# Scheduling ranks in a four-layer macaron network: routings and layer 0's attention 150 places ahead

## The chip, the cores and the metric
The kernel runs on one core of a Trainium2 chip. A core has five engines with a queue of instructions each: PE (TensorE, matmuls, with its weight loads shown as PEld), DVE (VectorE), ACT (ScalarE), POOL (GpSimd, which here issues the indirect gathers and scatters) and SP (SyncE, which issues the plain DMAs). The metric is the device time of one execution in microseconds (us), as the median over runs.

## The reference
Four sequences (batches 0 to 3) of 1024 tokens with 128 channels go through four layers, all in fp32. Each layer adds half a feed-forward block, an attention, and the same feed-forward block again. What matters here is layer 0 and layer 2, whose feed-forward blocks are mixtures of eight experts with two taken per token:

```python
x = x + 0.5 * _L0_ffn_ref(_layernorm(x), router_w, w1, b1, w2, b2)     # routed, GELU
x = x + _L0_attn_ref(_layernorm(x), Wq, Wk, Wv, Wfc)
x = x + 0.5 * _L0_ffn_ref(_layernorm(x), router_w, w1, b1, w2, b2)
x = x + 0.5 * _L1_ffn_ref(...)                                         # dense, SiLU
x = x + _L1_attn_ref(...)
x = x + 0.5 * _L1_ffn_ref(...)
x = x + 0.5 * _L2_ffn_ref(...)                                         # routed, ReLU
x = x + _L2_attn_ref(...)
x = x + 0.5 * _L2_ffn_ref(...)
...
# the routed block
logits = xf @ router_w.T
top_vals, top_idx = top_k(logits, 2); probs = softmax(top_vals)
for e in range(8):
    w = sum(where(top_idx == e, probs, 0))
    out += w * (act(xf @ w1[e].T + b1[e]) @ w2[e].T + b2[e])
# layer 0's attention: 16 heads of 8 channels, softmax over the heads of one token, not over tokens
scores = einsum('bshd,bstd->bsht', Q, K) / sqrt(8)
out = einsum('bsht,bstd->bshd', softmax(scores), V) @ Wfc.T
```

Layer 2's attention is a linear recurrence with a decay, layer 1's a softmax over 1024 tokens, layer 3 a recurrent mixer.

## The kernel before
The residual of each batch stays on the chip with channels on partitions (`X[b]`, 128x1024). A routed block is done in three kinds of tasks for a group of one or two batches.

- *Routing* (`route`, lines 276 to 421): normalizes the group's tokens, writes them as rows to DRAM (line 307), finds the two experts of each token, counts, and works out for every slot of every block which row it takes (`g_source`) and where its result goes (`g_target`, line 412, the last instruction). It is a chain of some 55 small DVE instructions, with matmuls and ACT work between. The eight `g_lanes` steps (line 399), with four matmuls each, are near its end.
- *Experts* (`experts`, lines 424 to 474): 23 blocks of 128 slots for one batch, 39 for two. For each block SP loads the expert's weights (`e_w`, four buffers), POOL gathers 128 rows (`e_xg`, line 457), PE transposes them (line 461), DVE copies them (`e_x`, line 463), PE multiplies up, ACT applies the activation (`e_h`, line 468), PE multiplies down, DVE adds the bias (`e_y`, line 441) and POOL scatters the result to DRAM (line 442).
- *Combine* (`combine`, lines 476 to 498), per batch: loads the two results of each token back (`c_y`, line 487), weighs and adds them (lines 492 and 493), transposes them (line 496) and adds half of them to the residual.

Layer 0's attention of a batch (`l0_attn`, lines 501 to 572) works on eight tiles of 128 tokens; each tile has four large DVE operations of 128x2048 elements (lines 528, 530, 545, 547) and some small ones, between a projection and a transposition on PE. Tasks are named after the round (0 before, 1 after the attention) and their first batch: route00, experts02, combine03. `middle0` to `middle3` are the attentions, `first` and `last` the dense feed-forward of layer 1 that is done inside the layers 0 and 2. In layer 0 the groups are (0), (1), (2, 3) in the first round and (0, 1), (2), (3) in the second; in layer 2 they are (0, 1) and (2, 3) both times.

The order of the work arises in two steps. `lanes` (line 1188) lays the tasks of several lanes out in turns: it always continues the lane whose clock of estimated costs is lowest, and begins a task when the tasks that it names are done. In layer 0 the lanes are: all experts; all combines; first routings, attentions and last feed-forwards; second routings. Then a list scheduler sets the order in each engine's queue at build time: among the instructions that it sees as ready it takes the one that was laid out first. The order in a queue is fixed from then on; semaphores do the waiting. Work of the routings, combines and attentions writes to the four PSUM banks of the pool `side`, the experts to the four of `main` (the first routing of each layer excepted).

Layer 1's attention has an order of PE written out by hand. The change does not touch it, nor layer 3.

Of the kernel before, what the change touches and what calls it, by code (L numbers as in the profile page):

```python
# [205 lines left out]
class Macaron:  # L206
# [981 lines left out]
    def lanes(self, *lanes):  # L1188
        lanes = [list(lane) for lane in lanes]
        clock, active, done = [0.0] * len(lanes), [None] * len(lanes), set()  # L1190
        while any(lanes) or any(active):
# [13 lines left out]
            else:  # L1205
                clock[n] += cost

    def macaron(self, name, moe, func, groups, marks, more):


        weights, (side, main), wp = self.packs[name + "m"], (self.side, self.main), self.fp
        plans = {}

        def plan(n, group):
            return plans.setdefault((n, group), {"mark": marks[n, group]})

        def route(n, group, *after, ps=side):
            return f"route{n}{group[0]}", after, lambda: self.route(ps, wp, moe, group, plan(n, group))

        def experts(n, group):  # L1220
            names = (f"route{n}{group[0]}",)
            return f"experts{n}{group[0]}", names, lambda: self.experts(main, wp, weights, func, group, plan(n, group))

        def combine(n, group):
            for b in group:
                yield f"combine{n}{b}", (f"experts{n}{group[0]}",), lambda b=b: self.combine(side, wp, group, b, plan(n, group))

        every = [(n, group) for n in range(2) for group in groups[n]]
        blocks = [experts(*g) for g in every]
        back = [task for g in every for task in combine(*g)]  # L1230
        self.lanes(blocks, back, *more(route))

    def layer0(self, moe, m, right, enter, ffn):
        m["wqkvc"] = self.centered(m["wqkv"], 3 * D)
        pa, pf = enter(right, "l0a"), enter(right, "l1f0")
        side, main = self.side, self.main

        def more(route):
            attn = lambda b, *after: (f"middle{b}", after, lambda: self.l0_attn(side, pa, m, b))
            last = lambda b, ps: (f"last{b}", (f"combine1{b}",), ffn(pf, ps, b))  # L1240
            return (
                [
                    route(0, (0,), ps=main), route(0, (1,)), route(0, (2, 3)),
                    *[attn(b, f"combine0{b}") for b in range(B)],
                    last(0, side), last(1, side), last(2, side), last(3, main),
                ],
                [route(1, (0, 1), "middle0", "middle1", "combine03"), route(1, (2,), "middle2"), route(1, (3,), "middle3")],
            )


        groups = [(0,), (1,), (2, 3)], [(0, 1), (2,), (3,)]
        marks = {(0, (0,)): "_1", (0, (1,)): "_2", (0, (2, 3)): "_0", (1, (0, 1)): "_0", (1, (2,)): "_1", (1, (3,)): "_2"}
        self.macaron("l0", moe, AF.Gelu, groups, marks, more)
# [118 lines left out]
```

## Time and profile before

| what | us |
|---|---|
| median of 3 runs | 3209.11 (3207.99 to 3214.21) |
| the profiled execution | 3296.3, its span 3294.4, mean granted PE clock 0.905 |
| layer 0 | from 0 to 945 |
| layer 1's attention | from 945 to 2038 |
| layer 2 | from 2038 to 2806 |
| layer 3 | from 2806 to the end |

The tasks of layers 0 and 2 in this execution, by the first and last DVE instruction of each:

| layer 0 | us | layer 2 | us |
|---|---|---|---|
| experts00 | 50 to 145 | route00 | 2098 to 2154 |
| experts01 | 143 to 235 | experts00 | 2159 to 2291 |
| middle0 | 177 to 300 | route02 | 2150 to 2215 |
| experts02 | 233 to 387 | experts02 | 2290 to 2451 |
| middle1 | 313 to 427 | route10 | 2431 to 2476 |
| combine03 | 407 to 413 | combine03 | 2480 to 2489 |
| route10 | 442 to 515 | experts10 | 2480 to 2647 |
| middle2 | 434 to 567 | route12 | 2602 to 2650 |
| experts10 | 517 to 670 | experts12 | 2654 to 2781 |
| middle3 | 582 to 729 | combine13 | 2798 to 2802 |
| route12 | 595 to 644 | | |
| experts12 | 667 to 783 | | |
| route13 | 756 to 791 | | |
| experts13 | 797 to 898 | | |

Whole-span busy shares are averages over stretches with different limits, and the kernel does little that the whole span could explain. The stretch is the unit to read: which engine is busy in it, and for what the engine that should be busy waits. The page's 40 slices show where such stretches begin:

```profile
PE   6888637878879999999999999988988977899997
DVE  3376877774226676676776772431555521355664
PEclk7989858889977999999999999979989988788997
```

Each digit is the busy share of 82 us in tenths, in the last row the PE clock that was granted.

### The profile page before, as it was taken

The page shows a single profiled execution, that of the slowest core. Times are in us where ns is not written, and L with a number is a line of the kernel's source. Part 1 is how long each engine was busy: PE and PEld are TensorE (multiplying, and loading weights), DVE is VectorE, ACT ScalarE, POOL GpSimd, SP SyncE. Part 2 cuts the span into 40 slices and gives each one's busy share as a digit, 9 for nine tenths or more (in the row PEclk, how much of TensorE's full clock was granted, in tenths as well). Part 3 has the DMA queues.
Part 4 walks back from the last instruction along what each step waited for, and adds up shares of the span by engine and source line. Part 5 has one row for each costly group of instructions (what it writes and reads, how often), then busy time and mean ns, then how long its engine had stood idle before and what let it go on. Part 6 is the DMA issues. An engine that isn't in the chain of part 4 may idle for free.

```text
span 3294.4 us, 48535 instructions
## 1 busy us (share of the span) xinstructions
PE 2875.3 (87%) x18206; PEld 1685.8 (51%) x18206; DVE 1826.5 (55%) x3160; ACT 1649.2 (50%) x3640; POOL 807.0 (24%) x748
## 2 busy tenths in 40 slices
PE   6888637878879999999999999988988977899997
PEld 6766426766643333333333333586777865344333
DVE  3376877774226676676776772431555521355664
ACT  3565524658613565566566565444444534444442
POOL 2565405552340000000000000046434454011110
PEclk7989858889977999999999999979989988788997
DMA  4766414663500000000000000157565666000000
GB/s 151 227 186 188 140 42 130 185 188 115 168 9 7 4 6 4 6 6 4 21 5 6 1 1 9 42 152 245 171 185 147 199 197 194 0 0 0 7 7 13
DMA packets 122890, 277.64 MB, mean 84 GB/s; under 512 B 18016, under 2 KB 67296, under 8 KB 122528
## 3 DMA queue, kind: packets, MB, share of 16 engines
q1 hardware_dynamic: 101792, 231.77, 23.8%
q0 software_dynamic: 20864, 42.77, 4.3%
q8 instruction: 144, 2.36, 0.3%
q14 instruction: 90, 0.74, 0.1%
HBM read 238.43 MB, written 31.85 MB: 82 GB/s over the span
## 4 chain that ended last, share of the span: by engine, by line
PE 74%; DVE 12%; ACT 5%; issue 4%; DMA 3%; POOL 1%; another core or an unknown queue 0%; SPq 0%; ACTq 0%; DVEq 0%; POOLq 0%
PE bank L227 40%; PE two L227 17%; PE o L227 8%; PE s L227 4%; DVE nm L720 2%; ACT e_h L468 2%; PE wave L1010 1%; DVE prod L545 1%; PE bank L461 1%; DMA c_y<-res 1%; DVE sc L530 1%; ACT L468 1%; DMA e_w<-in_l0m_dram 1%; DVE prod L528 1%; DVE e_x L463 1%
## 5 line engine op out<-in xcount | busy, mean ns | idle before, releaser
L720 DVE TENSOR_REDUCE nm<-two 128x2 f32<-128x1024 f32 x512 | 626.9, 1225 | 288.3 <-PE s L227 268.9
L743 ACT ACTIVATE e<-s 128x512 f32<-128x512 f32 x1024 | 556.4, 595 | 405.6 <-PE s L227 402.6
L468 ACT ACTIVATE e_h<-bank,e_w 128x128 f32<-128x128 f32 x1304 | 454.8, 368 | 511.6 <-PE bank L227 388.4
L227 PE MATMUL bank<-e_x,e_w 128*128 128x128 f32 x2608 | 569.3, 318 | 154.5 <-ACT e_h L468 79.9
L227 PE MATMUL s<-qm,kz 32*128 32x512 f32 x2048 | 634.1, 643 | 0.8 <-ACT e L743 0.8
L227 PE MATMUL two<-kz,qz 32*128 32x512 f32 x2048 | 593.2, 664 | 21.3 <-DVE nm L720 2.5
L227 PEld LDWEIGHTS bank<-e_x,e_w 128*128 128x128 f32 x2608 | 413.9, 204 | 291.3 <-ACT e_h L468 144.4
L457 POOL DMA_INDIRECT e_xg<-rows,g_source x326 | 334.4, 1026 | 835.1 <-DVE g_target L412 354.2
L227 PE MATMUL bank<-e_w,e_h 128*128 128x128 f32 x2608 | 445.7, 291 | 12.3 <-ACT e_h L468 6.9
L442 POOL DMA_INDIRECT res<-e_y,g_target x326 | 373.5, 1146 | 337.0 <-DVE e_y L441 152.7
L227 PEld LDWEIGHTS bank<-e_w,e_h 128*128 128x128 f32 x2608 | 378.8, 205 | 23.0 <-ACT e_h L468 13.3
L227 PE MATMUL o<-e,va 128*32 128x256 f32 x4096 | 328.8, 392 | 0.1
L441 DVE TENSOR_TENSOR e_y<-bank,e_w 128x128 f32<-128x128 f32 x326 | 94.3, 290 | 403.7 <-PE bank L227 317.0
L227 PEld LDWEIGHTS two<-kz,qz 32*128 32x128 f32 x2048 | 159.7, 189 | 239.9 <-issue 164.0
L227 PEld LDWEIGHTS o<-e,va 128*32 128x32 f32 x4096 | 81.0, 108 | 390.3 <-issue 370.3
L227 PEld LDWEIGHTS s<-qm,kz 32*128 32x128 f32 x2048 | 206.9, 183 | 10.9 <-issue 7.7
L708 POOL COPY va<-vd 128x256 f32<-128x256 f32 x16 | 6.7, 433 | 626.3 <-PE o L227 538.0
L1115 POOL TENSOR_TENSOR z<-st,r 128x512 f32<-128x512 f32 x32 | 46.2, 1445 | 417.1 <-DVE st L1108 333.7
L463 DVE COPY e_x<-bank 128x128 f32<-128x128 f32 x326 | 93.0, 285 | 92.2 <-PE bank L461 67.6
L227 PE MATMUL bank<-g_cols,g_lanes 128*128 128x39 f32 (+1 forms) x512 | 90.5, 341 | 28.9 <-DVE g_cols L392 28.8
L461 PE MATMUL bank<-c,e_xg 128*128 128x128 f32 x326 | 95.0, 291 | 21.7 <-DMA e_xg<-rows,g_source 21.6
L227 PEld LDWEIGHTS bank<-g_cols,g_lanes 128*128 128x128 f32 x512 | 91.2, 270 | 32.5 <-issue 31.4
(300 smaller groups left out, 3694.0 us busy)
## 6 DMA issues: line engine op xcount, KB each, us to landing
e_w<-in_l0m_dram SPq DMA_DIRECT2D x170, 578.0 KB
e_w<-in_l2m_dram SPq DMA_DIRECT2D x156, 578.0 KB
c_y<-res SPq DMA_DIRECT2D x32, 512.0 KB
rows<-g_xt SPq DMA_DIRECT2D x16, 512.0 KB
e_xg<-rows,g_source POOLq DMA_INDIRECT x326
res<-e_y,g_target POOLq DMA_INDIRECT x326
x<-in_x_dram SPq DMA_DIRECT2D x4, 512.0 KB
qz<-qd SPq DMA_DIRECT2D x64, 32.0 KB
```

The lines of the kernel that those rows point to most:

```text
L227: self.nc.tensor.matmul(out, lhsT, rhs, start=start, stop=stop)
L441: nc.vector.tensor_tensor(y, o, w[:, MOE_W - D :], ALU.add)
L442: ins = nc.gpsimd.indirect_dma_start(out=res[:, :], out_offset=at(target[:, k : k + 1]), in_=y, in_offset=None)
L457: nc.gpsimd.indirect_dma_start(out=xg, out_offset=None, in_=rows[:, :], in_offset=at(source[:, k : k + 1]))
L461: nc.tensor.transpose(tp, xg, self.c0["ident"])
L463: nc.vector.tensor_copy(x, tp)
L468: nc.scalar.activation(h[:, fc, :], up[:, fc, :], func, bias=w[:, 2 * FC * P + fc : 2 * FC * P + fc + 1])
L528: v.tensor_tensor(pr, q.unsqueeze(2).to_broadcast(sh), k.unsqueeze(1).to_broadcast(sh), ALU.mult)
L530: v.tensor_reduce(sc, pr, AX.X, ALU.add)
L720: v.tensor_reduce(nm[:, it, h, 2 * pair : 2 * pair + 2], s, AX.X, ALU.max, negate=True)
L743: nc.scalar.activation(es[g], s, AF.Exp, scale=scale)
L1115: (pool if i else v).tensor_tensor(z, st[:, 0:HALF], r, ALU.mult)
```

## The change
A helper wraps a task so that every step of it is laid out under a rank 150 places ahead of where it stands: the scheduler treats its instructions as though they had been laid out 150 instructions earlier. Two kinds of tasks are wrapped: all routings (layers 0 and 2), and layer 0's attentions. Experts, combines, layer 2's attentions and the dense feed-forwards keep their places. A block of the experts is some 19 instructions, so 150 places are nearly eight blocks. `lanes` itself lays out the same sequence as before, since the wrapper hands the costs through.

```diff
+    def ahead(self, task, offset):
+
+        while True:
+            with self.tc.high_priority(offset=offset):
+                cost = next(task, None)
+            if cost is None:
+                return
+            yield cost
+
     def macaron(self, name, moe, func, groups, marks, more):
...
         def route(n, group, *after, ps=side):
-            return f"route{n}{group[0]}", after, lambda: self.route(ps, wp, moe, group, plan(n, group))
+            return f"route{n}{group[0]}", after, lambda: self.ahead(self.route(ps, wp, moe, group, plan(n, group)), 150)
...
         def more(route):
-            attn = lambda b, *after: (f"middle{b}", after, lambda: self.l0_attn(side, pa, m, b))
+            attn = lambda b, *after: (f"middle{b}", after, lambda: self.ahead(self.l0_attn(side, pa, m, b), 150))
```

## The prediction

> **What bounds the kernel now.** The page comes first, and its 40 slices show two stretches that can move at all: layer 0 (0 to 945 us) and layer 2 (2038 to 2806 us). Layer 1's attention between them is ordered by hand, and layer 3 keeps its order: of its DVE instructions one moves, by two places.
>
> Second view, the busy time of each engine by stretch. Columns: stretch, length, busy us (instructions) of PE, PEld, DVE, ACT and POOL, granted PE clock, DMA share, GB/s.
> ```profile
> 177.00:427.00 250.00, 175.62 (x1040) 140.70 (x1040) 200.29 (x294) 140.28 (x325) 135.81 (x104) 0.86 0.54 164
> 427.00:515.00 88.00, 42.42 (x167) 34.01 (x165) 62.90 (x97) 23.06 (x72) 1.96 (x2) 0.54 0.12 40
> 515.00:797.00 282.00, 228.74 (x1369) 186.57 (x1370) 187.55 (x381) 182.52 (x421) 152.70 (x127) 0.90 0.59 175
> 2080.00:2159.00 79.00, 77.58 (x340) 55.63 (x338) 35.65 (x88) 38.97 (x113) 3.87 (x4) 0.85 0.16 53
> 2159.00:2291.00 132.00, 109.88 (x740) 95.62 (x738) 37.48 (x132) 59.89 (x175) 79.67 (x80) 0.94 0.70 211
> 2450.00:2480.00 30.00, 17.10 (x77) 15.68 (x76) 16.59 (x45) 4.91 (x16) 4.97 (x5) 0.54 0.51 158
> 2645.00:2660.00 15.00, 7.55 (x46) 6.54 (x46) 3.16 (x12) 1.72 (x6) 8.80 (x9) 0.68 0.67 185
> ```
> From 177 to 427 us (attention of batches 0 and 1 beside the experts) DVE is the limit, 200 of 250 us. From 427 to 515 us no experts run: their next group waits for its routing, as POOL's gather queue says:
> ```profile
> POOL e_xg L457 <- DVE g_far L410: 124.7, 1, 124.7
> ```
> In layer 2 PE is the limit, with holes where a group of experts has ended and the next routing has not: 2450 to 2480 and 2645 to 2660 us, both at a low granted clock.
>
> Third view, groups of DVE rows from 177 to 427 us (busy, mean ns, idle before and its ender). A large attention operation is 2.2 to 2.3 us, an expert's copy or add under 0.3 us, and the add is what DVE waits at:
> ```profile
> L545 DVE TENSOR_TENSOR prod<-ex,qkv 128x2048 f32<-128x2048 f32 x16 | 35.8, 2240 | 0.0
> L441 DVE TENSOR_TENSOR e_y<-bank,e_w 128x128 f32<-128x128 f32 x56 | 15.9, 287 | 29.7 <-PE bank L227 29.5
> L463 DVE COPY e_x<-bank 128x128 f32<-128x128 f32 x54 | 15.4, 285 | 5.6 <-PE bank L461 5.3
> ```
> Fourth, DVE in order of time. The last add of an expert group, then the first multiply of the combine that reads that group: 11.8 us apart (batch 1), and 9.3 us (batch 2).
> ```profile
> 235.10 0.29 DVE L441 TENSOR_TENSOR e_y<-bank,e_w 128x128 f32<-128x128 f32 x1 [1.26 <-PE bank L227]
> 246.91 1.93 DVE L493 SCALAR_TENSOR_TENSOR c_y<-c_y,g_p,c_y 128x128 f32<-128x128 f32 x7 [1.32 <-DMA c_y<-res]
> ...
> 386.42 0.28 DVE L441 TENSOR_TENSOR e_y<-bank,e_w 128x128 f32<-128x128 f32 x1
> 395.68 1.66 DVE L493 SCALAR_TENSOR_TENSOR c_y<-c_y,g_p,c_y 128x128 f32<-128x128 f32 x6 [1.55 <-DMA c_y<-res]
> ```
>
> **What the Trainium skill says.** "Perfetto Trace Analysis", Sequencer Loop: an engine reads its next instruction, and that one waits for its semaphores. So the order built into a queue holds even where a later instruction is ready; the 29.5 us at L441 agree. The same page, Optimization Strategy: stretches with different most-contended engines gain by being interleaved; 427 to 515 us (DVE alone) is such a stretch. "TensorE: Matmul & The Clock Gate", What's actually happening: PE's clock falls to half after an idle window of about 3.4 us; the 0.54 at 2450 us agrees.
>
> **The change part by part.** Nothing is computed differently. DVE has 3160 instructions in both builds, PE 9490 matmuls, POOL 748; ACT table loads go from 203 to 198. What changes is the order in each queue, so I compared the built orders and summed, from the trace of before, the durations of what stands ahead of each milestone.
>
> *B, 177 to 427 us: +20 us.* On DVE, attention overtakes experts: ahead of experts01's last add stand 60.5 us of batch 0's attention (before: 43.9), ahead of experts02's last add 72.0 us of batch 1's (58.0). Work up to batch 1's last DVE instruction stays 290.3 us, counted from the start, of which 69.5 lie ahead of batch 0's first (now 68.2). So attention itself comes no earlier; experts come later. And combines are not ranked: in the new PE order the next attention matmuls stand directly behind combine01's transposes, since they share the four side banks. On DVE the order now reads: attention, then 14 expert instructions with no attention among them, then combine01, then attention. Price of this pause: about three blocks to experts01's last add at the pace of the 300 to 316 us stretch (5 copies in 16 us, 3.2 us each), 9.6 us, plus 11.8 us to the combine, minus 14 x 0.286 = 4.0 us of work: 17 us idle. Behind the waiting transposes PE's queue also holds experts02's next matmuls, so that group stands still for the end of the pause. The second pause, 10 expert instructions before combine02: 3.5 x 3.2 + 9.3 - 2.9 = 17 us. Against it: before, DVE idled 250 - 220.8 = 29 us (sum of durations); a third of the 29.7 us at L441 should go, as adds now stand further behind their matmuls (-10), and batch 0's first large operations follow at once on its reciprocal (-5). Idle 29 + 34 - 15 = 48, work 222, together 270 against 250. Bounds: +5 if blocks stand ready and each pause is half as long, +35 if nothing of the 15 comes back.
>
> *C, 427 to 515 us: -6 us.* Route10 ends behind the same 68 to 70 us of DVE work. Its third instruction started at 458, behind 14.8 us of work in 31 us: it waited. Now 29.1 us of attention stand ahead of it, which use that time; I put it at 39 us. The 40.6 us left, at the old pace (54.2 us took 57), take 43: 82 against 88. Bounds -10 and +4.
>
> *D, 515 to 797 us: -6 us.* Before, experts12's last add is at 782.9, route13's last instruction at 791.2 and experts13's first copy at 797.3. In the new order route13 ends ahead of experts12's last add, so 14 us become one block's pitch: -11. A third pause of 14 expert instructions (before combine10) and 18.7 us more DVE work ahead of experts10's last add cost, but that stretch has DVE busy 188 of 282 us, and experts run on in the pause: +5. The five table loads saved (1283 ns each by the trace, on an engine with slack) are counted at nothing. Bounds -14 and +8.
>
> *E, 2080 to 2291 us: -11 us.* Route00 took from 2084 (its first ACT instruction) to 2154; routings with PE nearly free took 56 (2420 to 2476) and 58 us (2592 to 2650). In the new order it stands ahead of the ffn, with 27 us less PE and 10.5 us less DVE work before its end: experts00 starts 12 us earlier. (PE work: each matmul at its mean busy time in layer 2's full-clock stretches, 0.34 us for an up-projection of an expert, 0.23 us for a down-projection.) About 26 us of PE work move into its 132 us, where PE was busy 110; it just fits, so +1. Bounds -20 and -4. SP's rows transfer of route02 drops behind ten weight loads; experts02 need it 100 us later.
>
> *F, 2291 to 2806 us: -11 us.* Route10's last 21 us (2454 to 2475) ran at the low clock between two combines. Now the last blocks of experts02 stand between its instructions and combine02 and combine03 behind it: PE keeps its clock, about -8. What was late becomes the combines, 13 us of PE work later, and with them batches 2 and 3; that nearly uses up the 7 us hole between experts10's last add (2646.5) and experts12's first copy (2653.9), which closes: -3. Bounds -20 and -2.
>
> Sum: 20 - 6 - 6 - 11 - 11 = -14 us on the profiled execution's 3296.3 us. That one is 87 us (2.7%) over the median of 3209.11; I take the difference over unchanged: 3195.
>
> **Rivals.** *Combines hold up attention for longer (slower).* One mechanism: attention ranked ahead delays the expert group whose combine it must then wait for in PE's order. For it: DVE is the limit in B, and no rank helps the combines. Against it: DVE has 29 us idle there now. With B at +35, D at +5 (third pause), C 0, E -8, F -7: +25, 3234. It decides once the two pauses leave DVE idle over 48 us together; up to there the gains of C to F cover it.
> *The pauses are covered (faster).* Blocks stand ready behind attention and run through fast: B 0, C -8, D -12, E -13, F -13: -46, 3163. For it: POOL and DMA are half idle in B. Against it: 9 to 12 us from last add to combine are waits for transfers, which no order shortens.
> *The order moves and the end does not.* Routings are chains of small steps with their own length (56 to 58 us), so E and F give 5 each and B takes 10: 3209. Against it: C, D and F have visible holes.
>
> **How the numbers follow.** Chances: forecast 0.49, own range 3180 to 3213; slower rival 0.31; covered pauses 0.14; no effect 0.06. A measurement tells 0.2% (6.4 us) from no change. Faster by more: 0.33 + 0.14 + 0.01 = 0.48; within: 0.12 + 0.01 + 0.04 = 0.17; slower: 0.04 + 0.30 + 0.01 = 0.35. The range 3163 to 3236 leaves out the outer half of each outer rival, about 0.2.
>
> **What would show it.** B: experts02's last add near 405 to 420 us (before 386), and two stretches without attention on DVE, ended by L493. C: route10 from barrier to end in 82 us. D: experts13's first copy within 4 us of experts12's last add. E: experts00's first copy near 2147 less the shift of layer 0. F: no slice with half clock between experts02 and experts10. It is wrong if B costs more than all the others give, or if experts00 of layer 2 does not start earlier.

## The result, and the profile after

| kernel | median us | runs | span of the profiled execution |
|---|---|---|---|
| before | 3210.51 (3207.99 to 3214.21) | 4 | 3294.4 |
| after | 3290.28 (3280.79 to 3291.35) | 4 | 3287.5 |

The ratio is 1.0241 [1.0219, 1.0263]: the change makes the kernel about 80 us slower. The two spans say the opposite, minus 7 us. The profiled execution of before took about 80 us more than its timed ones, as every execution of this kernel did on the chip of experiments e1 to e4, nearly all of it where experts run, so times below are compared on one chip, and the trace of after (3289.27 us) is laid beside a later trace of the unchanged kernel (experiment e9, 3223.28 us, 7 us over the median on its chip).

The page of after, the same rows of the 40 slices as shown of before:
```profile
PE   6877745879878999999999999999998987899997
DVE  3376768674324676676677674333564622355664
PEclk8788856879876999999999999989999988888997
```
The barrier of layer 0 is the stretch before the end of route10 in which no experts run. Its low clock lies later than before, 5 and 6 in the slices from 411 to 575 us where it was 5 and 8, since the barrier itself has moved from 427 to 452 us. The busy time by stretch shows where the time went. Columns as before: stretch, length, busy us (instructions) of PE, PEld, DVE, ACT and POOL, granted PE clock, DMA share, GB/s. First the unchanged kernel (e9), cut at its own milestones:
```profile
165.80:413.00 247.20, 172.58 (x1039) 138.61 (x1039) 200.06 (x292) 139.67 (x325) 134.50 (x104) 0.87 0.55 166
413.00:496.70 83.70, 38.06 (x167) 30.98 (x165) 62.12 (x96) 22.89 (x72) 1.67 (x2) 0.58 0.12 42
496.70:774.00 277.30, 228.69 (x1371) 187.30 (x1372) 188.34 (x385) 182.35 (x421) 151.67 (x128) 0.89 0.59 178
774.00:913.40 139.40, 122.79 (x596) 84.74 (x595) 39.15 (x94) 82.51 (x152) 41.43 (x43) 0.89 0.36 109
2015.00:2130.30 115.30, 113.65 (x459) 74.41 (x459) 50.45 (x112) 48.46 (x130) 3.89 (x5) 0.90 0.12 39
2130.30:2238.80 108.50, 103.76 (x741) 90.42 (x741) 37.57 (x133) 58.95 (x174) 80.12 (x80) 0.99 0.84 258
2238.80:2426.10 187.30, 166.19 (x1116) 144.43 (x1114) 102.32 (x320) 83.78 (x256) 73.28 (x76) 0.91 0.60 184
2426.10:2591.50 165.40, 154.12 (x1103) 135.59 (x1103) 95.56 (x302) 75.21 (x225) 79.35 (x80) 0.97 0.61 181
2591.50:2726.80 135.30, 108.80 (x694) 89.87 (x694) 33.37 (x123) 64.78 (x188) 73.14 (x75) 0.88 0.73 219
```
Then after, cut at the same milestones: the first attention's start; the barrier before route10; route10's end; experts13's first copy; the end of layer 0; and in layer 2 first1's start, experts00's first copy and last add, experts10's first copy, experts12's first copy, combine13's end.
```profile
170.40:451.60 281.20, 197.83 (x1096) 157.31 (x1094) 202.21 (x296) 149.29 (x340) 132.15 (x110) 0.81 0.49 153
451.60:533.60 82.00, 38.26 (x146) 31.47 (x146) 62.94 (x96) 20.65 (x68) 1.71 (x2) 0.52 0.13 43
533.60:820.70 287.10, 233.13 (x1355) 192.22 (x1355) 186.91 (x372) 174.31 (x408) 143.95 (x125) 0.84 0.54 166
820.70:973.10 152.40, 127.21 (x609) 87.96 (x609) 42.88 (x104) 84.98 (x161) 43.61 (x45) 0.85 0.37 112
2074.60:2173.80 99.20, 90.69 (x348) 58.09 (x347) 43.22 (x98) 33.37 (x84) 4.66 (x5) 0.85 0.12 41
2173.80:2305.00 131.20, 125.41 (x850) 104.23 (x850) 45.67 (x149) 69.67 (x216) 78.07 (x80) 1.00 0.68 218
2305.00:2476.60 171.60, 157.29 (x1108) 136.17 (x1106) 98.40 (x310) 79.27 (x240) 71.54 (x74) 0.98 0.58 182
2476.60:2662.40 185.80, 167.01 (x1107) 147.00 (x1105) 96.63 (x313) 79.04 (x240) 81.41 (x83) 0.92 0.54 170
2662.40:2796.80 134.40, 106.87 (x702) 88.46 (x702) 33.67 (x120) 64.62 (x190) 72.05 (x74) 0.90 0.73 232
```
Line by line, the first stretch is 34 us longer with the same DVE work (200 against 202 us), the second 2 shorter, the third 10 and the fourth 13 longer. In layer 2 the stretch before experts00 is 16 us shorter and experts00 itself 23 longer; the next is 16 shorter, experts10's 20 longer, and the last about the same. With 4.6 us ahead of the first line and 3.9 us less in layer 3 this is the 66 us between the two spans. The medians differ by 77 to 80 us; most of the rest is that e9's execution lies over its median.

**Layer 0, attention of batches 0 and 1.** The DVE rows of that stretch (busy, mean ns, idle before and its ender), first of e9, then of after:
```profile
L441 DVE TENSOR_TENSOR e_y<-bank,e_w 128x128 f32<-128x128 f32 x56 | 15.9, 285 | 27.2 <-PE bank L227 27.1
L463 DVE COPY e_x<-bank 128x128 f32<-128x128 f32 x54 | 15.2, 282 | 4.5 <-PE bank L461 4.2
L493 DVE SCALAR_TENSOR_TENSOR c_y<-c_y,g_p,c_y 128x128 f32<-128x128 f32 x24 | 6.9, 345 | 3.5 <-DMA c_y<-res 3.5
```
```profile
L545 DVE TENSOR_TENSOR prod<-ex,qkv 128x2048 f32<-128x2048 f32 x16 | 36.1, 2256 | 0.0
L441 DVE TENSOR_TENSOR e_y<-bank,e_w 128x128 f32<-128x128 f32 x59 | 16.8, 287 | 50.4 <-PE bank L227 48.2 <-DMA res<-e_y,g_target 2.0
L463 DVE COPY e_x<-bank 128x128 f32<-128x128 f32 x57 | 16.1, 282 | 8.4 <-PE bank L461 8.1
L493 DVE SCALAR_TENSOR_TENSOR c_y<-c_y,g_p,c_y 128x128 f32<-128x128 f32 x24 | 6.8, 345 | 11.6 <-DMA c_y<-res 11.6
```
The attention itself runs as fast as before, 2.2 to 2.3 us for a large operation without a wait (L545). Idle at the three other rows goes from 35.2 to 70.4 us, about the whole loss of the stretch. Where it sits is seen in order of time; DVE in after, the end of the second pause:
```profile
411.63 0.29 DVE L441 TENSOR_TENSOR e_y<-bank,e_w 128x128 f32<-128x128 f32 x1 [2.07 <-PE bank L227]
414.02 0.29 DVE L441 TENSOR_TENSOR e_y<-bank,e_w 128x128 f32<-128x128 f32 x1 [2.10 <-PE bank L227]
422.87 1.93 DVE L493 SCALAR_TENSOR_TENSOR c_y<-c_y,g_p,c_y 128x128 f32<-128x128 f32 x7 [8.55 <-DMA c_y<-res]
```
No attention stands between 398.6 and 426.7 us: six adds of experts02 follow each other at 2.5 us, then 8.6 us go by until combine02's transfers have landed. DVE is idle for 22.8 of these 28 us, and for 16.8 in the first such pause (242.0 to 265.4). In e9 the same two places have one pause with 3.9 us of idle time. PE, in after, at the end of the pause:
```profile
423.28 1.52 PE L496 MATMUL bank<-c,c_y 128*128 128x128 f32 x5 [9.29 <-DVE c_y L493]
424.60 1.49 PE L227 MATMUL bank<-cw,x 128*128 128x384 f32 x2
```
The transposes of the combine wait 9.3 us at the head of the queue, and attention's next projection is directly behind them.

The combine is late because its experts are, and one thing that puts the experts back can be read directly: their copies (`e_x`, L463) now stand behind attention's large operations in DVE's queue. PE's waits for them over layer 0, from the first attention on (us in total, times, longest), of e9 and then of after:
```profile
PE bank L227 <- DVE e_x L463: 21.0, 19, 2.5
PE bank L227 <- DVE e_x L463: 51.5, 30, 7.5
```
The longest follows the barrier. The first block of experts10 is transposed at 534.6 us, but its copy starts at 545.3, behind nine operations of attention, and PE idles for 7.5 us of that time; in e9 the copy starts 1.2 us after the transposition.
```profile
545.62 0.79 PE L227 MATMUL bank<-e_x,e_w 128*128 128x128 f32 x2 [7.48 <-DVE e_x L463]
```

**Where gaps closed.** The same wait turns up where the prediction saw gains. PE in after, a few us after experts13's start in layer 0, and after experts10's in layer 2:
```profile
833.72 1.26 PE L496 MATMUL bank<-c,c_y 128*128 128x128 f32 x4 [7.55 <-DVE c_y L493]
...
2493.91 1.26 PE L496 MATMUL bank<-c,c_y 128*128 128x128 f32 x4 [7.70 <-DVE c_y L493]
```
The gaps before the two groups have gone, and so has the time in which a combine's transfers could land unnoticed: at 833.31 us DVE has waited 8.2 us for them, and experts' matmuls stand behind the transposes until 834.77, though three blocks had been copied by 825.1. Nor had the gap before experts13 been free on PE, which was busy for 11.8 of its 15.5 us in e9.

POOL's gathers at the barrier still wait for route10's end, 116.3 us (124.7 in the first profile, 121.3 in e9).

### The profile page after: what moved, and what is told of

It is laid out like the page before. It is cut to its first block, busy times and chain, and to the rows that moved or that the text cites. A ratio compares the mean times of both kernels' runs of the same rounds, so it can differ in the third digit from the quotient of the medians.

```text
span 3287.5 us, 48548 instructions
## 1 busy us (share of the span) xinstructions
PE 2886.5 (88%) x18206; PEld 1695.9 (52%) x18206; DVE 1828.3 (56%) x3160; ACT 1639.7 (50%) x3635; POOL 788.3 (24%) x748
## 3 DMA queue, kind: packets, MB, share of 16 engines
q1 hardware_dynamic: 101792, 231.77, 22.8%
## 5 line engine op out<-in xcount | busy, mean ns | idle before, releaser
L227 PE MATMUL bank<-e_x,e_w 128*128 128x128 f32 x2608 | 579.0, 321 | 141.9 <-DVE e_x L463 60.1
L442 POOL DMA_INDIRECT res<-e_y,g_target x326 | 353.9, 1086 | 359.6 <-DVE e_y L441 135.4
L441 DVE TENSOR_TENSOR e_y<-bank,e_w 128x128 f32<-128x128 f32 x326 | 94.1, 289 | 368.6 <-PE bank L227 356.0
L463 DVE COPY e_x<-bank 128x128 f32<-128x128 f32 x326 | 92.2, 283 | 67.7 <-PE bank L461 66.1
```

What stands on the lines that cost most here:

```text
L227: self.nc.tensor.matmul(out, lhsT, rhs, start=start, stop=stop)
L441: nc.vector.tensor_tensor(y, o, w[:, MOE_W - D :], ALU.add)
L442: ins = nc.gpsimd.indirect_dma_start(out=res[:, :], out_offset=at(target[:, k : k + 1]), in_=y, in_offset=None)
L463: nc.vector.tensor_copy(x, tp)
```

## The experiments

Each edit is shown against before unless it says otherwise; `ahead` is the wrapper of the change. Ratios are to before on the same chip.

**e1_unchanged.** No edit.

> The kernel before itself, unchanged, with its profile. In the two profiles the changed kernel is 7 us shorter (span 3287.5 against 3294.4), in the timed runs 80 us longer. Theory 1 (two speeds): a build runs at one of two speeds some 85 us apart, whatever its order; the timed runs of before were fast and its profiled one slow. Then this profile may come out near 3210, and its stretches show where the 85 us lie. Theory 2 (the order): before is truly 3210 and the profiler slows it by 87 us; then time near 3210 and span near 3294 again. Rival: the time is a matter of the chip, then 3290 here.

3291.66 us over 12 runs, before 3291.25; ratio 0.9998 [0.9976, 1.0019]. The shown profile of before (3296.3) was thus no odd execution. The difference does not go with the build: the unchanged kernel takes 3291 us here, on chip 0, and 3215 us in e5 to e15, on chips 1, 4 and 9. Of the first runs the chip is not on record. Each chip was used in one session only, so that chip and session are not told apart.

**e2_routes_only, e3_attn_only, e4_layer2_only.** One kind of the change alone: all routings; layer 0's attentions; layer 2's routings.
```diff
-lambda: self.l0_attn(side, pa, m, b)                                      # e3
+lambda: self.ahead(self.l0_attn(side, pa, m, b), 150)
-lambda: self.route(ps, wp, moe, group, plan(n, group))                    # e2; e4 only if name == "l2"
+lambda: self.ahead(self.route(ps, wp, moe, group, plan(n, group)), 150)
```


> Only the routings are ranked 150 ahead, layer 0's attention is not. By order: layer 2 as in the changed kernel (36 us shorter in the profile), layer 0 without the overtaking by attention, so about 0 to +5: span near 3262. Theory 1: time either near its span (3262) or 85 us below it (3177). Theory 2, the order of attention costs the time: 3210 - 36 + 5 = 3179.

> Only layer 0's attention is ranked 150 ahead. By order: layer 0 about 30 us longer in the profile, layer 2 as before: span near 3325. Theory 1: time near 3325 or near 3240. Theory 2, attention's order costs 80 us or more in timed runs: 3290 to 3330.

> Only layer 2's four routings are ranked 150 ahead; layer 0 is as before. By order: 36 us shorter: span near 3258. Theory 1: time 3258 or 3173. Theory 2, layer 0's order carries the loss: 3174.

On the chip of e1: routings 3320.15, ratio 1.0086 [1.0054, 1.0119]; attentions 3341.27, 1.0148 [1.0114, 1.0182]; layer 2's routings 3295.37, 1.0005 [0.9988, 1.0023]. None of them is where an expectation had it, and neither kind gains. What the two kinds cost adds up to 2.34%, near the change's own 2.41%. Layer 2 shows neither the predicted gain nor a loss here.

**e5_after_here.** The whole change again.

> The whole change, beside the kernel before on the chip of the first four runs. Theory 1 (layer 0 carries the loss: +50 us by the attention's rank and +29 us by the routings' rank, layer 2 nothing): the same ratio as at first, 1.024, so about 3370 us (3358 to 3382) beside a before of 3291, and in its trace layer 2, from the first DVE instruction of first1 to the last of combine13, at 750 to 770 us instead of 722. Rival (the parts do not add up, or the change costs less where transfers are slow): under 3350 us.

The unchanged kernel takes 3215.43 us on this chip, the changed one 3292.44, ratio 1.0242 [1.0215, 1.0269]. The ratio repeats. Layer 2 took 730 us from first1 to combine13, not the 750 to 770 that were expected beside a before of 3291. The late first copy of experts10 repeats too (10.7 us after its transposition).

**e6_combines_too.** The whole change, and layer 0's combines ranked as well; against after:
```diff
-lambda b=b: self.combine(side, wp, group, b, plan(n, group))
+lambda b=b: self.ahead(self.combine(...), 150) if name == "l0" else self.combine(...)
```


> The whole change, and layer 0's combines ranked 150 places ahead as well. Theory 1 (a combine waits for the last block of its experts, and attention behind it waits for the side banks, which are handed out in the order in which the work was laid out; rank changes neither): the time of the whole change within 12 us (3358 to 3382), the two pauses of DVE near 240 and 400 us as long as before (23 and 28 us). Rival (the prediction's: the pauses come from combines without a rank beside attention with one): the pauses halve and 20 to 40 us come back, 3330 to 3350.

3304.65 us, ratio 1.0281 [1.0264, 1.0298]: 12 us more than the whole change, and pauses of 24.5 and 33.4 us (23.4 and 28.1 in after). A combine without a rank is not what makes the pauses. It waits for the last block of its experts and then for its transfers; a rank speeds up neither. That the order in which the side banks are handed out ties attention to it is argued from the built order, not shown by itself.

**e7_attn01_only and e13_attn23_only.** The attentions of two batches alone.
```diff
+lambda: self.ahead(self.l0_attn(side, pa, m, b), 150) if b < 2 else self.l0_attn(side, pa, m, b)   # e13: b > 1
```


> Only the attentions of batches 0 and 1 are ranked ahead; those of 2 and 3 and all routings are not. Theory 1 (two of the three pauses, 40 of 57 us of idle DVE, belong to these two): 30 to 38 us of the 50 us that ranking all four cost, 3321 to 3329 beside 3291; experts10 to experts13 keep their 380 us. Rival (the second half of layer 0 carries the loss, because attention overtakes experts10 there): under 3310.

> Only the attentions of batches 2 and 3 are ranked ahead. Theory 1 (one long pause of DVE, before combine10, instead of two; experts beside attention are put back as in the first half): 8 to 20 us over before, so that the five parts (attention 0 and 1 +25, attention 2 and 3, layer 0's routings +30, layer 2's two rounds +10 and +3) sum to the 77 us of the whole change within 12 us. Rival (only the first half suffers): within 6 us of before.

Batches 0 and 1: 3240.07, 1.0078 [1.0061, 1.0095]. Batches 2 and 3: 3239.91, 1.0075 [1.0053, 1.0096]. Each half costs about 25 us; together they give e3's 1.5%. Both expectations missed, the first too high and the second too low: the trace of e13 has one pause (24.9 us, 18.2 idle, before combine10) and loses as much as the two of e7; there experts10 takes 156 us (149 in e9), experts13 101 (95), and route10 81 instead of 72, so more than the pauses is at work in the second half. PE's waits for experts' copies come to 33.8 us over layer 0 in e13 and to 27.2 in e7, against 21.0 in e9.

**e8_attn_40.** Layer 0's attentions ranked by 40 places.
```diff
+lambda: self.ahead(self.l0_attn(side, pa, m, b), 40)
```


> Layer 0's attentions ranked 40 places ahead instead of 150, no routing ranked. In the built order combine01 then stands among attention's instructions, without a stretch of experts alone before it; the second such stretch shrinks from 10 expert instructions to 1. Theory 1 (the cost of the rank is the pauses, where attention has run as far as its banks let it and then waits for a combine that waits for experts which were put back): at most 20 us over before, 3285 to 3311. Rival (each place that attention overtakes experts costs, pauses or not): 3318 to 3340.

3219.69 us over 20 runs, 1.0022 [1.0009, 1.0036]. Of the 1.5% that 150 places cost, 0.2% are left. DVE rows of the same stretch:
```profile
L441 DVE TENSOR_TENSOR e_y<-bank,e_w 128x128 f32<-128x128 f32 x56 | 16.0, 286 | 29.9 <-PE bank L227 29.8
L463 DVE COPY e_x<-bank 128x128 f32<-128x128 f32 x54 | 15.4, 284 | 4.7 <-PE bank L461 4.6
L493 DVE SCALAR_TENSOR_TENSOR c_y<-c_y,g_p,c_y 128x128 f32<-128x128 f32 x24 | 7.1, 346 | 6.3 <-DMA c_y<-res 6.0 <-ACT c_y L492 0.3
```
40.9 us idle against 70.4 in after and 35.2 in e9; the first pause is gone, the second has 7.1 us of idle time. The loss goes with the pauses, and with PE's waits for experts' copies: over layer 0 these are 14.5 us here, 21.0 in e9 and 51.5 in after. No run separates the two. It does not go with PE's waits for the combines, which are 35.1 us here, 13.7 in e9 and 36.9 in after. Attention is still ranked ahead of two blocks of experts; that much costs little. A cost in proportion to the places would have been 0.4%, outside the interval.

**e9_before_again.** No edit; for its trace.

> The kernel before once more, for its trace. Where a run of it takes about 3215 us (as on the second chip session) and not 3291 (as on the first), Theory 1 says that the missing 75 us lie in the stretches in which experts run beside little else: layer 2 from first1 to combine13 near 706 us (758 in the profile shown at first), its experts00 near 108 us instead of 132 and near 103 us of PE work in it; layer 1's attention and layer 3 the same within 3 us. Rival: every stage is faster by the same share.

3223.28 us, beside a before of 3215.98. From first1 to combine13 712 us (758 in the first profile); experts00 of layer 2 takes 108.5 us with PE busy for 103.8, where the first profile had 132 and 110; layer 1's attention is the same. The shorter time lies mostly with the experts, as expected (at the barrier it is 4 us), and with it goes the slack of PE on which step E was built.

**e10_l2_round0 and e11_l2_round1.** Layer 2's routings of one round alone.
```diff
+lambda: self.ahead(self.route(...), 150) if name == "l2" and n == 0 else self.route(...)    # e11: n == 1
```


> Only layer 2's two routings of the first round are ranked ahead. Theory 1 (experts00 is bound by PE once its transfers keep up; starting it 12 us earlier puts the rest of the dense feed-forward, some 22 us of PE work, inside it): 8 to 16 us over before where before takes about 3215 us, within 8 us of it where before takes about 3291. Rival (the prediction: that work just fits): 6 to 12 us below before.

> Only layer 2's two routings of the second round are ranked ahead. Theory 1 (the idle PE of 2451 to 2480 us is traded for the wait of combine02's transposes for their transfers, 7.7 us in the changed kernel; the hole before experts12 closes, but experts10 takes the work that the two stretches gave up): within 6 us of before. Rival (the prediction): 6 to 14 us below before.

Round 0: 3226.41, 1.0041 [1.0021, 1.0061]. Round 1: 3219.17 over 20 runs, 1.0015 [1.0004, 1.0026]. Experts00 in e10, by stretch:
```profile
2111.00:2243.10 132.10, 125.36 (x850) 104.31 (x851) 45.78 (x149) 69.58 (x216) 76.94 (x78) 1.00 0.70 215
```
It starts 14 us earlier after first1 than in e9 (101.0 against 115.3) and takes 23.6 us longer, with 21.6 us more PE work in it. PE is busy for 95% of it both times: the work does not fit, it adds.

**e12_l0_routes and e14_l0_round1.** Layer 0's routings alone; then only those of the second round.
```diff
+lambda: self.ahead(self.route(...), 150) if name == "l0" else self.route(...)               # e14: and n == 1
```


> Only layer 0's routings are ranked ahead. Theory 1 (routings of layer 0 mostly have time; ranked ahead they stand before the experts' copies and adds, whose blocks set the pace): 15 to 30 us over before, spread over experts01, experts02, experts12 and experts13; where before takes about 3215 us the sum of this run and of the two layer 2 runs, less three times before, comes to what the change costs beyond attention. Rival (layer 2 carries the 29 us that ranking all routings cost): within 6 us of before.

> Only layer 0's three routings of the second round are ranked ahead. Theory 1 (route13 ends earlier and experts13 follows experts12 without a gap, but the dense feed-forwards last0 and last1 are pushed from beside experts12 to beside experts13, as first3 is in layer 2, and route12 stands ahead of experts10's blocks): 8 to 18 us over before, experts13 10 us longer (95 before), the rest of the 30 us of all of layer 0's routings being route02's. Rival (the prediction): 6 to 12 us below before, from route10 and the closed gap.

All of them: 3245.62, 1.0099 [1.0073, 1.0125]; against e9, experts01 is 4 us longer, experts02 9, experts12 8, experts13 12. The second round alone: 3228.70, 1.0042 [1.0030, 1.0054]. There experts13's first copy follows experts12's last add by 0.7 us (15.5 in e9), and experts13 takes 109 us instead of 95. The reason put down beforehand for that is wrong: the dense feed-forward has the same 72 matmuls in it as before. PE busy rises by 5.5 us, and PE idle from 4.6 to 13.1: it waits 4.6 us for combine12's transposes and 4.8 us for the group's weights (1.2 in e9). The gap had been covering both. So closing it gains nothing: from experts12's last add to experts13's last add it is 110.0 us against 110.8 in e9. What e14 loses lies one group earlier, from experts10's last add to experts12's: 121.4 us against 110.7, with PE busy for 101.8 instead of 89.7, as the work that had filled the gap moves in there (PE was busy in it for 11.8 us, and is now for 0.7).

The five parts (0.78, 0.75, 0.99, 0.41 and 0.15%) sum to 3.08%, against 2.42% for the whole change. By the medians that is 16 us more, where agreement within 12 us was expected, and 0.66% is more than the intervals taken together in quadrature (0.5%). The parts do not simply add: the 10 us that experts12 loses in e12 and e14 are absent from the whole change (107.1 us), while experts10's first copy comes 10.7 us after its transposition only in the kernels that rank both kinds (after, e5, e6), and within 1.3 us of it in all others.

**e15_experts_ahead.** The other way round: experts ranked 20 places ahead, nothing else.
```diff
-lambda: self.experts(main, wp, weights, func, group, plan(n, group))
+lambda: self.ahead(self.experts(main, wp, weights, func, group, plan(n, group)), 20)
```


> The other way round: all experts of layers 0 and 2 are ranked 20 places (one block) ahead, routings and attentions not at all. Theory 1 (who is put back loses; experts pass through all engines and set the pace): experts' stages get 5 to 10 us shorter beside attention, attention as much longer, together -15 to +10 us. Rival (any rank that pulls kinds of work apart loses, since the laid-out order already mixes DVE work and PE work as the stretch needs): over +15 us.

3245.61, 1.0094 [1.0063, 1.0124]. Experts02 ends 10 us earlier than in e9 (362.8 against 372.5), batch 1's attention no earlier (414.4 against 413.0), and middle3 ends 25 us later. The rival's number holds: experts gain less than the others lose. No version tried is faster than before.

## Why the prediction was wrong

| step | predicted us | after less e9 us |
|---|---|---|
| B, attention of batches 0 and 1 | +20 | +34 |
| C, route10 at the barrier | -6 | -2 |
| D, to experts13's first copy | -6 | +10 |
| experts13 to the end of layer 0 | not counted | +13 |
| E, to the end of layer 2's experts00 | -11 | +7 |
| F, the rest of layer 2 | -11 | +4 |

The steps forecast -14 us and the two traces show +66. The prediction's own sign of being wrong came true: B costs more than all the others give. Apart from B's two pauses, the steps counted what the ranked work gains and put what happens to the work behind it at little or nothing; these are the terms that failed.

**B: mechanism right, one credit wrong.** The two pauses came where they were foretold, ended by L493. Experts02's last add came at 414 us (405 to 420 predicted), but that is partly luck: after's first attention starts 7 us earlier than in the profile that the forecast was counted on, and measured from there the add is 34 us later, not 18 to 33. That combines lack a rank is not the reason (e6); the loss goes with how far the experts are put back (e8). Priced at 17 us of idle time each, they measured 16.8 and 22.8. The term that failed is the 15 us set against them: "a third of the 29.7 us at L441 should go" and batch 0's first operations following at once. Outside the pauses DVE idles before these adds for 26.6 us in after and for 26.1 in e9, so none of that third came back: the adds still wait for PE. Of all its idle time outside the pauses 39.4 us are left against 43.2, so that about 4 of the 15 us came back. The 29 us of idle DVE from which the step starts are too few as well: summed durations count overlaps twice, and the busy column gives 250 less 200, 50 us.

**C: right in the end point, by luck.** From the barrier 82 us were predicted and 82.0 measured. Of these, 39 were forecast up to route10's third instruction and 43 after it; it was 33.9 and 48.1, two misses of 5 us that cancel. And the 88 it started from is 83.7 in e9, so the gain was mostly never there.

**D: the gap closed as predicted, and was given back twice.** Experts13's first copy follows experts12's last add by 2.1 us instead of 15.5. The term that failed is the +5 for the third pause and the DVE work put ahead, since "experts run on": experts10's first copy comes 11.7 us after route10's end (2.3 in e9), experts10 then takes 166 us (149), and only experts12 is 4 us shorter, +23 in all. The third pause has 17.7 us of idle DVE (6.0 in e9's pause there). And step D stopped at experts13's first copy: after it PE waits 7.55 us for combine12, which the closed gap no longer hides.

**E: the step that failed is "it just fits, so +1".** Experts00 does start earlier, by 16 us after first1 (12 predicted), and 22 us of PE work move into it (26 predicted). Experts00 grows by 23 us. The forecast's own figures did not fit, 110 + 26 = 136 us of PE work in 132, and its room was that of the profile of 3296 us; in e9 it is 108.5 less 103.8. The page of the Trainium skill that the prediction named, "Perfetto Trace Analysis", Optimization Strategy, says that performance may be improved by interleaving regimes with different most-contended engines, which is less than the gain that the prediction took from it; here both are PE's, 113.7 of 115.3 us and 103.8 of 108.5. Round 0 alone costs 10 to 13 us (e10). On the chip of e1, where the room was larger, layer 2's ranking cost nothing, but it did not gain either (e4), and in e4's trace experts00 takes 145.8 us, against 132.1 in the first profile and 128.4 in e1: the work did not just fit there either. The profiled execution's distance of 87 us from the median had been noted ("I take the difference over unchanged"); it should have been looked for by stretch, since it was the very slack that E spends.

**F: a wait exchanged for another.** Route10's low-clock tail did go: PE idles 14.3 us in the stretch before experts10 instead of 21.1. Combines did become late, with 12.9 us more PE work in experts10's stretch (13 predicted). What was left out is that their transposes stand in PE's queue ahead of the experts' matmuls and wait there for their own loads: 7.70 us in one place. PE's idle time over both stretches is 33.1 us, against 32.4 in e9. The prediction named them ("What was late becomes the combines"), but did not ask what they wait for.

The slower rival had B right in size (+35 against +34) and by its mechanism, attention ahead of the experts whose combine it then waits for. But it was to decide from 48 us of idle time in the two pauses, and there were 39.6; it too let E and F gain, and stood at 3234. The larger part of the miss is that the gains of C to F, 34 us in the prediction, turned into 19 us of cost, and that 13 us came in a stretch that was not looked at.

## What to carry to other kernels

An order that mixes work for different engines is a balance: to rank one kind of work ahead is to rank all others back, and with the order fixed at build time whatever waits for the work put back holds up all that stands behind it in its queue; ranking that task ahead too did not help here (e6). Before a gap is counted as a gain, list what lands or loads during it, and which engines work in it. Before work is moved into another stretch, take that stretch's room from an execution as fast as the timed ones, and a small offset may do what a large one cannot (40 places 0.2%, 150 places 1.5%).

## What was not expected of the hardware

The same program takes 3291 us on one chip and 3215 us on three others, each in a session of its own, with layer 1's attention unchanged (1101.6 us from the end of layer 0 to first1 in e9, 1101.8 in the first profile). In experts00 of layer 2, 211 GB/s were moved in the first profile and 258 in e9, at DMA shares of 0.70 and 0.84, so the DMA engines are busy for about the same time per byte in both; what makes the blocks follow each other more slowly in the first profile stays open.
